# Seven block products for layer 0's attention output too, and one place for the attention weights, in a two-layer diffusion transformer kernel

## The chip, the cores and the metric

The kernel runs on one core of one Trainium2 chip. The metric is device microseconds for one execution. Before the change three runs took 2224.48, 2226.77 and 2225.25 us: the median is 2225.25 us. A core has five engines that run their own instruction queues side by side: TensorE (PE, with PEld for its weight loads), VectorE (DVE), ScalarE (ACT), GpSimd (POOL) and SyncE (SP), which issues all DMA transfers of this kernel. An instruction that waits for a semaphore holds up all that stands behind it on its engine.

## The reference

Two transformer layers over a batch of 16 items, each 256 rows of 256 numbers, all in fp32. Layer 0 (`D` = 256, 16 heads of 64) is self attention, cross attention over a context of 256 rows of 192, and a feed-forward net; each adds to `x`:

```python
attn_in = _adaln(x, cond, ln1_w, ln1_b, g1_w, g1_b, b1_w, b1_b)
x = _attn(attn_in, attn_in, sa_wq, sa_wkv, sa_wo, sa_bo) + x
cross_in = _adaln(x, cond, ln1_w, ln1_b, g1_w, g1_b, b1_w, b1_b)
ctx_n = _ln(context, ca_lnc_w, ca_lnc_b)
x = _attn(cross_in, ctx_n, ca_wq, ca_wkv, ca_wo, ca_bo) + x
ffn_in = _adaln(x, cond, ln2_w, ln2_b, g2_w, g2_b, b2_w, b2_b)
h = jax.nn.gelu(ffn_in @ ff_w1 + ff_b1, approximate=False)
x = h @ ff_w2 + ff_b2 + x
```

`_attn` projects to queries, keys and values of width 1024 (`MID`), turns queries and keys by a rotary embedding, takes softmax and sums over values, and ends with `o @ wo + bo`, where `o` is 256 x 1024 and `wo` 1024 x 256. That last product is what the change is about. Layer 1 does the same kinds of steps with heads of 16 and another modulation; there the attention output product is 256 x 256 by 256 x 256 and stays as it is.

## The kernel before

There are six phases: layer 0 self attention, cross attention and FFN, then the same three of layer 1. In each phase all 16 items are worked through, one after another; an item is a "job". An attention job has two steps (s = 0 and 1, eight heads each in layer 0), an FFN job four. The queues are in the order in which the kernel issues the instructions: no scheduler reorders them, and the program's tile framework adds the semaphores.

The loop over steps (from L861) writes the order by hand. In a layer 0 attention step it has, in this order: VectorE's partial sums of the exponentials (`stage_t`, tile `both`, L548; `stage_turn`, L554), TensorE's projections for the next step, called `rotary`, four pieces of which VectorE multiplies by the rotary table into the tiles `m` (L484) and POOL combines pairwise into `qk` (L492); then the sums over values (`layer0_sums`, L596), `stage_reduce` (L561), the rest of the previous job, the next job's values (`layer0_values`, L82 and L431) and at the end the next scores (`stage_s`, L527), whose exponentials ACT takes (L539). The tiles `m` have two buffers each, so VectorE's m for the second half of a step wait for POOL's qk of the first.

The previous job is called `late`. In step 0 its softmax sums are added up (`sum_up`), inverted, and sent through DRAM to be spread over partitions (tile `spread`); in step 1 POOL multiplies the job's four raw sums by them (`scale`, L585), and TensorE makes the output product (`finish`, L724, recorded at the helper's line L82): eight chunks by two row tiles into one PSUM bank, and one VectorE add into `x` (L738). PSUM has eight banks, addressed by number; rotary uses 0 to 3, the sums 4 and 5, values 6 and 7, scores 0 to 7, and `finish` bank 1. The next scores therefore begin, in bank 0, where rotary's products have been read.

The FFN's second product is 256 x 1024 by 1024 x 256 as well and is made by Strassen's scheme: `fold_weights` (L671) adds and subtracts blocks of the weight once a phase, `fold_hidden` (L684) makes five sums of blocks of the hidden activations on VectorE (L699), `finish_folded` (L701) does seven block products of 128 x 512 by 512 x 128 instead of eight, in two banks, and adds them into `x` with five VectorE instructions (L713 to L720). In each fp32 product a matrix instruction stands twice in the trace: 64 calls show as 128 records.

Weights lie in the pool `wpool`, two buffers for each of the tags `wq`, `wkv`, `wo`, `bo`. `load_phase` (L786) loads all weights of the next phase into the other buffers in step 1 of the first job of a phase (step 3 in an FFN).

Of the kernel before, what the change touches and what calls it, by code (L numbers as in the profile page):

```python
# [16 lines left out]
P = 128  # L17
# [26 lines left out]
def fast(ctx: ExitStack, tc: tile.TileContext, a: dict, out: bass.AP, flag):  # L44
# [166 lines left out]
    def wtile(shape, tag, name):  # L211
        return wpool.tile(shape, F32, tag=tag, name=name)

    def load_layer0_attention(kind, between=None):
        wq = wtile([P, KC, H * 64], "wq", f"wq_{kind}")
        wkv = wtile([P, 2, 2 * H * 64], "wkv", f"wkv_{kind}")
        wo = wtile([P, 8, D], "wo", f"wo_{kind}")
        halves = [slice(part * 512, (part + 1) * 512) for part in range(4)]

        def load_keys(cut):  # L220
            nc.sync.dma_start(out=wkv[:, :, cut], in_=chunked(a[f"{kind}_wkv"])[:, :, cut])

        def load_queries(cut):
            nc.sync.dma_start(out=wq[:, :, cut], in_=chunked(a[f"{kind}_wq"])[:, :, cut])

        load_keys(halves[0])
        load_queries(halves[0])
        if between is not None:
            between(0)
        load_keys(halves[2])  # L230
        load_keys(halves[3])
        if between is not None:
            between(1)
        load_queries(halves[1])
        load_keys(halves[1])
        bo = broadcast_row(a[f"L0_xcond_{kind}_bo"], "bo", f"bo_{kind}")
        nc.sync.dma_start(out=wo, in_=chunked(a[f"{kind}_wo"]))
        return {"wq": wq, "wk": wkv, "wv": wkv[:, :, H * 64 :], "wo": wo, "bo": bo}

    def load_layer1_self():  # L240
        w = wtile([P, KC, 3 * D], "wkv", "wqkv_b")
        nc.sync.dma_start(out=w, in_=chunked(a["L1_xcond_Wqkv"]))
        wo = wtile([P, KC, D], "wo", "wo_b1")
# [6 lines left out]
    def load_layer1_cross():  # L250
        w = wtile([P, 3, 2, D], "wkv", "wqkv_c")
# [3 lines left out]
        wo = wtile([P, KC, D], "wo", "wo_b2")  # L255
# [6 lines left out]
    def load_ffn(w1n, w2n, b1n, b2n, key):  # L262
        w1 = wtile([P, KC, 4 * D], "wq", f"w1_{key}")
        w2 = wtile([P, 8, D], "wo", f"w2_{key}")
        nc.sync.dma_start(out=w1, in_=chunked(a[w1n]))
        nc.sync.dma_start(out=w2, in_=chunked(a[w2n]))
        return {"w1": w1, "w2": w2, "b1": b1n, "bo": broadcast_row(a[b2n], "bo", f"bo_{key}")}
# [402 lines left out]

    def fold_weights(ph):  # L671
        w2 = ph["w"]["w2"]
        b = [[w2[:, 4 * k : 4 * k + 4, n * P : (n + 1) * P] for n in range(2)] for k in range(2)]
        folded = ph["folded"] = {2: b[0][0], 5: b[1][1]}
        for m, x, y, op in ((1, b[0][0], b[1][1], ALU.add), (3, b[0][1], b[1][1], ALU.subtract),
                            (4, b[1][0], b[0][0], ALU.subtract), (6, b[0][0], b[0][1], ALU.add),
                            (7, b[1][0], b[1][1], ALU.add)):
            folded[m] = (
                work.tile([P, 4, P], F32, tag="cT", name=f"folded_w_{m}") if m == 7 else
                work.tile([P, 4, P], F32, tag="qk", name=f"folded_w_{m}", bufs=4)  # L680
            )
            nc.vector.tensor_tensor(folded[m], x, y, op)

    def fold_hidden(job):  # L684
        a = [[job["halves"][k][:, :, t * P : (t + 1) * P] for k in range(2)] for t in range(2)]
        folded = job["folded"] = {3: a[0][0], 4: a[1][1]}
        sums = [
            (5, a[0][0], a[0][1], ALU.add), (2, a[1][0], a[1][1], ALU.add), (1, a[0][0], a[1][1], ALU.add),
            (7, a[0][1], a[1][1], ALU.subtract), (6, a[1][0], a[0][0], ALU.subtract),
        ]  # L690
        if job is jobs[-1]:
            sums = sums[4:] + sums[:4]
# [905 lines left out]
```

## Time and profile before

| What | Value |
|---|---|
| median of the runs | 2225.25 us (2224.48 to 2226.77) |
| profiled execution | 2226.61 us, of it span 2224.7 us |
| granted TensorE clock | 1.000 |
| one self attention job of layer 0 | 42.11 us (392.54 to 434.65) |
| one cross attention job of layer 0 | 39.37 us (884.84 to 924.21) |
| layer 0's two attention phases | about 31 to 1318 us of the span |
| POOL's scale, L585 | 128 instructions, 184.4 us, mean 1472 ns |
| VectorE's `both`, L548 | 256 instructions, 213.7 us; 624 / 684 / 1804 ns least, median, most |
| VectorE's FFN folds, L699 | 155 instructions, 674 / 683 / 879 ns |
| matrix product 128x32 by 128x256 | 379 ns in flight, four side by side |
| matrix product 128x32 by 128x128 | 273 ns in flight |

The page gives busy time for each engine, then the chain of waits that ended last, then groups of instructions by line. A group's mean can hide instructions that waited inside: `both` is one. The timeline lists an engine's instructions in order, equal neighbours merged ("x4"), with start and length in us; a remark in brackets tells how long the engine was idle before, and who released it. Matrix instructions overlap, so the time of a stretch of products is best taken from start to start.

### The profile page before, as it was taken

The numbers are of one execution on the slowest core, as the hardware profiler recorded it, in microseconds if no ns is written. First come the engines' busy times: TensorE is split into PE (matmuls) and PEld (weight loads), VectorE is DVE, ScalarE is ACT, GpSimd is POOL, SyncE is SP. The second block draws the span as 40 slices with busy tenths as digits, with TensorE's granted clock in tenths as the row PEclk, the third lists the DMA queues.
The fourth block names the chain that finished last, engine by engine and source line by source line (L and its number), as shares of the span: only waits on it lengthen the run. The fifth ranks groups of instructions, "written<-read, shape, count | busy, mean of one in ns | idle before, by whom it ended". The sixth has DMA issues, their size and how long they took to land.

```text
span 2224.7 us, 104669 instructions
## 1 busy us (share of the span) xinstructions
PE 2208.8 (99%) x47625; PEld 1401.1 (63%) x47625; DVE 1583.5 (71%) x2996; ACT 836.8 (38%) x1303; POOL 871.5 (39%) x873
## 2 busy tenths in 40 slices
PE   9999999999999999999999999999999999999998
PEld 5555555555555555555555567777665665657998
DVE  5777677677678787787878775564777777777654
ACT  2233233233233333333323332233666666663322
POOL 3445444445445546454554532121223322223220
PEclk9999999999999999999999999999999999999999
DMA  8110011111122221221212113211211232223221
GB/s 253 37 40 22 22 35 28 22 35 29 25 46 81 57 60 36 46 53 37 62 34 46 38 44 90 51 41 46 51 37 42 48 100 61 61 51 80 65 62 37
DMA packets 305678, 117.29 MB, mean 53 GB/s; under 512 B 242548, under 2 KB 288968, under 8 KB 305096
## 3 DMA queue, kind: packets, MB, share of 16 engines
q1 hardware_dynamic: 305224, 110.51, 20.5%
q8 instruction: 374, 6.13, 1.2%
q14 instruction: 80, 0.66, 0.1%
HBM read 77.14 MB, written 33.29 MB: 50 GB/s over the span
## 4 chain that ended last, share of the span: by engine, by line
PE 98%; POOL 1%; DVE 1%; issue 0%; ACT 0%; DMA 0%; SPq 0%; POOLq 0%; ACTq 0%; DVEq 0%
PE banks L82 64%; PE banks L527 16%; PE banks L596 10%; PE banks L612 5%; PE banks L463 2%; PE banks L431 1%; PE banks L171 0%; POOL raw L585 0%; DMA mod_a<-in_L_xcond_g_w 0%; POOL qk L492 0%; DVE m L484 0%; ACT pr L539 0%; DVE sums L638 0%; POOL oT L647 0%; ACT hT L356 0%
## 5 line engine op out<-in xcount | busy, mean ns | idle before, releaser
L539 ACT ACTIVATE pr<-banks 128x1024 f32<-128x1024 f32 x576 | 487.3, 938 | 220.8 <-PE banks L527 207.3
L492 POOL TENSOR_TENSOR qk<-m,m 128x512 f32<-128x512 f32 x256 | 347.0, 1376 | 370.5 <-DVE m L484 266.4
L484 DVE TENSOR_TENSOR m<-banks,rope 128x512 f32<-128x512 f32 x512 | 325.3, 681 | 89.0 <-POOL qk L492 74.2
L548 DVE TENSOR_TENSOR both<-pr 128x512 f32<-128x512 f32 x256 | 213.7, 844 | 75.0 <-ACT pr L539 73.7
L603 ACT COPY raw<-banks 128x512 f32<-128x512 f32 x128 | 75.0, 586 | 473.3 <-PE banks L596 400.7
L527 PE MATMUL banks<-qk 32*64 32x256 f32 x8192 | 238.7, 377 | 0.4 <-POOL qk L492 0.3
L527 PEld LDWEIGHTS banks<-qk 32*64 32x64 f32 x8192 | 184.4, 131 | 78.0 <-issue 44.0
L596 PE MATMUL banks<-pr,v 128*32 128x256 f32 x4096 | 233.4, 379 | 0.0
L662 ACT ACTIVATE g<-banks,cols 128x256 f32<-128x256 f32 x256 | 106.5, 470 | 278.3 <-PE banks L82 261.8
L436 ACT COPY v<-banks 128x512 f32<-128x512 f32 x128 | 71.8, 587 | 357.2 <-PE banks L431 178.8
L596 PEld LDWEIGHTS banks<-pr,v 128*32 128x32 f32 x4096 | 133.2, 110 | 88.5 <-ACT pr L539 0.7
L585 POOL TENSOR_TENSOR raw<-raw,spread 128x512 f32<-128x512 f32 x128 | 184.4, 1472 | 0.0
L554 DVE STREAM_TRANSPOSE squares<-both 128x1024 f32<-128x1024 f32 x128 | 159.1, 1243 | 3.4
L738 DVE TENSOR_TENSOR x<-banks,x 128x512 f32<-128x512 f32 x65 | 44.9, 691 | 158.9 <-PE banks L82 158.9
L561 DVE TENSOR_REDUCE rows<-squares 128x32 f32<-128x1024 f32 x128 | 155.4, 1214 | 2.2
L290 POOL TENSOR_TENSOR rstd<-ve,neg_half 128x2 f32<-128x2 f32 x95 | 67.0, 705 | 197.0 <-DVE ve L288 193.7
L82 PE MATMUL banks<-hT,wq_sa 128*32 128x256 f32 x2048 | 135.7, 381 | 2.3 <-issue 2.3
L82 PE MATMUL banks<-hT,wkv_sa 128*32 128x256 f32 x2048 | 136.2, 383 | 0.9 <-ACT hT L356 0.9
L612 PE MATMUL banks<-pr,wide_v 128*32 128x256 f32 x2048 | 134.4, 379 | 1.1 <-ACT pr L539 1.1
L82 PE MATMUL banks<-hT,wq_ca 128*32 128x256 f32 x2048 | 134.0, 379 | 0.0
L647 POOL TENSOR_TENSOR oT<-oT,spread 128x256 f32<-128x256 f32 x64 | 45.7, 735 | 209.9 <-DVE spread L646 209.9
L527 PE MATMUL banks<-q,k 32*64 32x256 f32 x4096 | 127.8, 381 | 0.0
(146 smaller groups left out, 3543.9 us busy)
## 6 DMA issues: line engine op xcount, KB each, us to landing
turned<-blocks SPq DMA_DIRECT2D x380, 64.0 KB
fetched<-turned SPq DMA_DIRECT2D x380, 64.0 KB
spread<-sums_seen SPq DMA_DIRECT2D x128, 128.0 KB
x<-in_x SPq DMA_DIRECT2D x16, 256.0 KB
fetched_c<-turned_c SPq DMA_DIRECT2D x64, 64.0 KB
cT<-in_ctx_turned SPq DMA_DIRECT2D x16, 256.0 KB
out<-x SPq DMA_DIRECT2D x16, 256.0 KB
ctx<-in_ctx SPq DMA_DIRECT2D x16, 192.0 KB
```

The source lines that it names most:

```text
L82: nc.tensor.matmul(out[cut], lhsT[:, cut], rhs, start=start, stop=stop)
L484: nc.vector.tensor_tensor(m, pq, rope[:, s : s + 1, :].to_broadcast([P, 2, N]), ALU.mult)
L492: nc.gpsimd.tensor_tensor(r, x, y, (ALU.subtract, ALU.add)[out])
L527: nc.tensor.matmul(banks[64 * g : 64 * g + 64, at + h, t * N : (t + 1) * N], lhs, rhs, start=(half == 0), stop=(half == 1 or job["layer"] ...
L539: nc.scalar.activation(pr[:, one], sc[:, one], AF.Exp, scale=0.125 if job["layer"] == 0 else 0.25)
L548: nc.vector.tensor_tensor(job["both"][:, 2 * p : 2 * p + 2, :], pr[:, :, 0, :], pr[:, :, 1, :], ALU.add)
L554: nc.vector.transpose(job["squares"].rearrange("p b k -> p (b k)"), job.pop("both").rearrange("p h n -> p (h n)"))
L561: nc.vector.tensor_reduce(job["rows"][:, u, :], job.pop("squares"), AX.X, ALU.add)
L585: nc.gpsimd.tensor_tensor(part, part, spread[:, u : u + 1, :].to_broadcast([P, 2, N]), ALU.mult)
L596: nc.tensor.matmul(o[32 * h : 32 * h + 32, half, :], v[:, t, col : col + 32], prs[h // 2][:, h % 2, t, :], start=(t == 0), stop=(t == NT - 1),
L612: nc.tensor.matmul(o[32 * h : 32 * h + 32], v[:, t, 4 * c + h, 32 * e : 32 * e + 32], prs[h // 2][:, h % 2, t, :], start=(t == 0), stop=(t ...
L662: nc.scalar.activation(g[:, c, :], ph[:, c, :], AF.Gelu, bias=column(w["b1"], 2 * u + c))
```

## The change

Layer 0's attention output product goes through `fold_weights` and `finish_folded` as well. The five folds of a job's sums are split: 5, 2 and 1 on POOL in step 0 of the next job, right after `scale`, which moves there from step 1; 7 and 6 on VectorE in step 1, between rotary's last two pieces. `finish_folded` uses banks 1 and 0 (7 and 6 in a phase's last job) and stands behind both of VectorE's reduces. An attention phase's weights are folded in step 0 of job 1, two on POOL and three on VectorE. The last cross attention job, which is finished inside the FFN, keeps `finish`.

The weights' tags become `wk`, `wq` and `wv` with one buffer each, shared by all phases; `wo` keeps two, and five folded weights get tiles of their own. Loads are in three parts: "early" (bias, output weights, modulation, all of layer 1's attention) in step 1 of job 1 (3 in an FFN), "values" at the start of step 0 of the phase's last job, "keys" (keys and queries, or the FFN's first weights) at the end of that step, ahead of the scores.

```diff
-    def load_layer0_attention(kind, between=None):
...
+    def load_layer0_attention(kind, part, between=None):
+        halves = [slice(i * 512, (i + 1) * 512) for i in range(4)]
+        wkv_src = chunked(a[f"{kind}_wkv"])
+        w = {}
+        if part == "keys":
+            w["wk"] = wtile([P, 2, H * 64], "wk", f"wk_{kind}")
+            w["wq"] = wtile([P, KC, H * 64], "wq", f"wq_{kind}")
+            for i, cut in enumerate(halves[:2]):
+                nc.sync.dma_start(out=w["wk"][:, :, cut], in_=wkv_src[:, :, cut])
+                nc.sync.dma_start(out=w["wq"][:, :, cut], in_=chunked(a[f"{kind}_wq"])[:, :, cut])
+                if between is not None and i == 0:
+                    between()
+        if part == "values":
+            w["wv"] = wtile([P, 2, H * 64], "wv", f"wv_{kind}")
+            for i in range(2):
+                nc.sync.dma_start(out=w["wv"][:, :, halves[i]], in_=wkv_src[:, :, halves[2 + i]])
+        if part == "early":
+            w["bo"] = broadcast_row(a[f"L0_xcond_{kind}_bo"], "bo", f"bo_{kind}")
+            w["wo"] = wtile([P, 8, D], "wo", f"wo_{kind}", 2)
+            nc.sync.dma_start(out=w["wo"], in_=chunked(a[f"{kind}_wo"]))
+        return w
...
     def fold_weights(ph):
-        w2 = ph["w"]["w2"]
...
-            nc.vector.tensor_tensor(folded[m], x, y, op)
+            if ph["kind"] == "attn":
+                folded[m] = wtile([P, 4, P], "folded", f"folded_w_{m}", 5)
...
+            (nc.gpsimd if ph["kind"] == "attn" and m < 4 else nc.vector).tensor_tensor(folded[m], x, y, op)
+
+    def fold_inner(job, eng, *which):
         a = [[job["halves"][k][:, :, t * P : (t + 1) * P] for k in range(2)] for t in range(2)]
...
+        folded = job.setdefault("folded", {3: a[0][0], 4: a[1][1]})
+        sums = {5: (a[0][0], a[0][1], ALU.add), 2: (a[1][0], a[1][1], ALU.add), 1: (a[0][0], a[1][1], ALU.add),
+                7: (a[0][1], a[1][1], ALU.subtract), 6: (a[1][0], a[0][0], ALU.subtract)}
+        for m in which:
+            folded[m] = work.tile([P, 4, P], F32, tag="folded", name=f"folded_{job['key']}_{m}", bufs=5)
+            eng.tensor_tensor(folded[m], *sums[m])
+
+    def finish_folded(job, at):
...
-        first, second = (bank(next_bank(), 4, P) for _ in range(2))
-        third = bank(next_bank(), 4, P) if final else second
+        first, second, third = (bank(i, 4, P) for i in (at if final else (*at, at[1])))
...
-        if s == (3 if ffn else 1) and job["b"] == 0 and job["p"] + 1 < len(phases):
-            load_phase(job["p"] + 1)
+        more = job["p"] + 1 < len(phases)
+        if s == 1 and job["b"] == (3 if ffn else 1) and more:
+            load_phase(job["p"] + 1, "early")
+        if s == 0 and job["b"] == NB - 1 and more:
+            load_phase(job["p"] + 1, "values")
...
-            if late is not None and s == 1:
-                scale(late)
...
             rotary(then, 1, 0)
+            if late is not None and s == 1:
+                fold_inner(late, nc.vector, 7, 6)
             rotary(then, 1, 1)
             for e in range(2):
                 layer0_sums(job, 2 * s + e, 4 + e if then else e)
             stage_reduce(job, 2 * s)
-            if late is not None and s == 1 and then:
-                finish(late, 1)
             stage_turn(job, 2 * s + 1)
             stage_reduce(job, 2 * s + 1)
-            if late is not None and s == 1 and not then:
-                finish(late, 7)
+            if late is not None and s == 1:
+                finish_folded(late, (1, 0) if then else (7, 6))
+            if late is not None and s == 0:
+                scale(late)
+                fold_inner(late, nc.gpsimd, 5, 2, 1)
+            if s == 0 and job["b"] == 1:
+                fold_weights(job["phase"])
...
+        if s == 0 and job["b"] == NB - 1 and more:
+            load_phase(job["p"] + 1, "keys")
         scores(i + 1)
```

The FFN's folds move to the new tiles too, in the order they had, and its first weights become the "keys" part of its phase.

## The prediction

> **What bounds the kernel now.** I read the page's busy shares and its chain of waits first, then the table by stretches for one item of each layer 0 attention phase, then the timeline of the steps that the change touches. Page:
>
> ```profile
> PE 2208.8 (99%) x47625; PEld 1401.1 (63%) x47625; DVE 1583.5 (71%) x2996; ACT 836.8 (38%) x1303; POOL 871.5 (39%) x873
> PE 98%; POOL 1%; DVE 1%; issue 0%; ACT 0%; DMA 0%; SPq 0%; POOLq 0%; ACTq 0%; DVEq 0%
> ```
>
> TensorE never waits in mid phase, so a shorter product shows in full unless another engine falls late. By stretches (one self attention item, one cross attention item; columns: length, then busy time of PE, PEld, DVE, ACT, POOL):
>
> ```profile
> 392.54:434.65 42.11, 42.11 (x844) 24.34 (x840) 29.41 (x44) 12.73 (x17) 19.51 (x16) 1.00 0.13 28
> 884.84:924.21 39.37, 39.37 (x796) 22.46 (x792) 31.13 (x53) 12.95 (x18) 20.98 (x18) 1.00 0.20 46
> ```
>
> VectorE is busy 70% of an item in self attention, 79% in cross attention: cross attention has less room. The timeline has the old product, the FFN's seven-product form of the same size, and the second step of a cross item:
>
> ```profile
> 1002.78 7.09 PE L82 MATMUL banks<-wo_ca,raw 128*32 128x256 f32 x128
> 1009.69 1.90 PE L82 MATMUL banks<-wkv_ca,cT 128*32 128x512 f32 x16
> ...
> 1350.58 1.93 PE L82 MATMUL banks<-w_a,folded 128*32 128x128 f32 x64
> 1352.33 1.93 PE L82 MATMUL banks<-folded_w,g 128*32 128x128 f32 x64
> 1354.08 2.80 PE L82 MATMUL banks<-folded_w,folded 128*32 128x128 f32 x96
> 1356.70 1.91 PE L82 MATMUL banks<-hT,w_a 128*32 128x256 f32 x32
> ...
> 987.26 2.52 POOL L492 TENSOR_TENSOR qk<-m,m 128x512 f32<-128x512 f32 x2 [1.49 <-DVE m L484]
> 993.89 5.65 POOL L585 TENSOR_TENSOR raw<-raw,spread 128x512 f32<-128x512 f32 x4
> 999.75 2.81 POOL L492 TENSOR_TENSOR qk<-m,m 128x512 f32<-128x512 f32 x2 [0.22 <-DVE m L484]
> ...
> 996.97 1.42 DVE L548 TENSOR_TENSOR both<-pr 128x512 f32<-128x512 f32 x1
> 999.51 0.67 DVE L548 TENSOR_TENSOR both<-pr 128x512 f32<-128x512 f32 x1
> 1001.36 2.53 DVE L484 TENSOR_TENSOR m<-banks,rope 128x512 f32<-128x512 f32 x4 [1.18 <-POOL qk L492]
> 1003.81 1.21 DVE L561 TENSOR_REDUCE rows<-squares 128x32 f32<-128x1024 f32 x1
> 1009.94 0.69 DVE L738 TENSOR_TENSOR x<-banks,x 128x512 f32<-128x512 f32 x1 [4.92 <-PE banks L82]
> ```
>
> Read three things. The old product takes 6.91 us (start to start). The FFN's seven products take 6.12 us. And POOL leaves the m buffers only when its qk pair runs, so VectorE's last four m wait for POOL; the `both` add takes 1.42 us instead of 0.67 us while POOL runs a two-input instruction.
>
> **The product.** 6.91 - 6.12 = 0.79 us for each of the 31 items that use the new form (self attention 0 to 15, cross attention 0 to 14; the last cross item keeps the old form). 31 x 0.79 = **24.5 us gained**.
>
> **The folds and the scaling, cross attention.** POOL's scale (4 instructions) moves from the second step to the first, ahead of it nothing but qk; behind it come three folds and the rstd pair, and only then the second step's qk. POOL's two-input 128x512 takes 1.26 us in qk, 1.47 us in raw beside VectorE, 1.24 us from start to start alone; the folds were never on POOL, so 1.24 to 1.47 us each, and I take 1.24 plus VectorE's turns. From 989.78 (end of qk): three scales to 993.55, `both` to 994.1, fourth scale to 995.25, `both` to 995.8, folds to 997.0, 998.2, 999.45, the third `both` to 1000.0. On VectorE: transpose to 997.05, m to 998.3, m after the third `both` to 1001.2. POOL's rstd pair ends 1001.3, so qk starts at 1001.4 (before: 999.75) and frees the first buffer at 1002.95. Then VectorE in its new order: two m 1.22, folds 7 and 6 (0.60 apart; 0.68 each in the FFN) 1.20, two m 1.2, reduce 1.24, transpose 1.28, reduce 1.14, that is 1010.3; then the five adds, which in the FFN take 2.35 us without waits: 1012.65. They read banks 1 and 0, and the next scores begin by writing bank 0. TensorE is ready at 1002.78 + 6.12 + 2.85 (values) = 1011.75, and must wait until 1012.7: **0.95 us per item**, which eats the 0.79. Queued behind the wait are the scores, ACT's exponentials and all of the next step, so it is paid in full: 13 steps (in cross items 0 and 3 to 14) x 0.95 = **12.4 us**. The one in item 2 has 1.9 us of modulation products as cover: 0.2. Bounds for one item: without contention 0; with folds at 1.47 us, 1.6.
>
> The row for that contention is `both` at 1.42 against 0.67 us: it waits 0.75 us. [...]
>
> **The same in self attention.** There POOL's qk ends 1.39 us before the scores instead of 0.36 us after them, values take 3.55, and the rstd is one. The same replay leaves qk's start at 388.6 (before 388.88), VectorE is done with its reduces at 397.6, before TensorE's product ends at 398.5; the last two adds end at 399.7 and the scores are ready to start at 402.0. 2.2 us of cover once VectorE's own chain is counted, so no cost; the cover is gone if POOL or VectorE comes more than that later.
>
> **The weights' folds** stand in the first step of item 1: two on POOL (2.5 us) and three on VectorE (0.6 to 1.23 us each: 1.8 to 3.7) behind the scale. They delay qk by 3.4 us (self) and 4.0 us (cross): 3.4 - 2.2 = 1.2 us, and 0.95 + 4.0 = 5.0. **6.2 us** (bounds 2 and 9: the instructions hidden as in the FFN, or each at its longest).
>
> **One place for the weights.** Loads now wait until the place is free. (a) Self to cross: the values' half goes out at about 664 in the last self item and lands some 5 us later, in time for 669.55. The keys' loads stand behind sums, spread and fetch on SP, which end at 673.8 before, and later by about 2.4 us since 1 MB is in front of them: first 512 KB issued at 676.2. Before, such a load landed 4.3 to 4.8 us after issue; the first use (cross keys, right after the scores) was at 676.04. Wait 680.5 - 676.04 = **4.5 us** (bounds 2.5 and 6). Queries come 1.3 us behind, as they are used. (b) Cross to FFN: 1 MB issued about 1304.5, needed at 1318: nothing. But POOL's folds there end after the scale that already held TensorE at 1314.16 (0.61 us): the last finish gains nothing, **1.0 us** with that. (c) Cross to FFN in layer 1: the load stands behind the four sums_seen issues, needed by the FFN's first product:
>
> ```profile
> 2001.94 2.49 SPq L642 DMA_DIRECT2D sums_seen<-sums  x4
> 2006.14 5.36 PE L82 MATMUL banks<-hT,w_b 128*32 128x256 f32 x96
> ```
>
> Issued at 2004.45. The FFN's 1 MB load of 715.64 moved its last bytes in the fifth microsecond and landed 5.2 us after issue: 2009.65, so **3.5 us** of idle TensorE (bounds 2.5 and 5). [...]
>
> SP's other moved loads (the output weights in item 1 of the phase before, 1 MB, no longer 4.5 MB in item 0) lie beside 40 us of work. The end of the kernel and the FFN's folds keep order and length; only their buffers change.
>
> **Sum.** -24.5 + 12.4 + 0.2 + 6.2 + 4.5 + 1.0 + 3.5 = +3.3 us. On the profiled execution, 2226.61 us (span 2224.7 and 1.9 around it), that is 2229.9; it lay 1.36 us over the median of the three runs, so **2228.5 us**.
>
> **Rivals.** (1) The cross attention chain is in time: if POOL's folds and `both` fall so that qk starts 1 us sooner, 12.4 us are saved: **2216**. For it: the chain misses by under 1 us in 22. Against: both POOL and VectorE reach 1001.3 on their own. (2) POOL's folds read strided halves and run slower, the trace has none like it: at 1.47 us (its mean raw) to 1.77 (its slowest qk) instead of 1.24 the chain is 0.6 to 1.6 us longer in cross attention, while self attention is still covered: 14 x 0.6 to 1.6 = 8 to 22 us more, **2237 to 2250**. It decides from folds of 1.34 us on. Against: qk and raw of equal size take 1.24 alone. (3) The loads are earlier than I think, SP not held up: 8 us fewer, **2221**. (4) The product does not shorten: against it, the FFN's identical 224 matrix products take 6.12 us; no chance of note.
>
> **How the numbers follow.** Forecast as reckoned 0.5, own range 2223 to 2235 (waits 0.6 to 1.3 us for 13 items, loads 5 to 11 us); rival 1 0.2; rival 2 0.2; rival 3 0.1. The range 2215 to 2239 holds the forecast, rivals 1 and 3 and the near part of 2. A measurement of this kernel tells about 0.2% (4.45 us) from no change: below 2220.8 is faster, above 2229.7 slower. Faster: 0.2 from rival 1 and 0.04 from 3. Same: 0.28 of the forecast, 0.06 of 3. Slower: 0.22 of the forecast and 0.2.
>
> **What the profile would show.** Right: groups of 128x128 products for wo at 6.12 us; a self attention item of 41.3 us; a cross item of 39.5 us with scores waiting on VectorE's last add; gaps of some 4 us ahead of the first cross keys and 3.5 us ahead of the second FFN. Wrong: cross items of 38.6 us (rival 1) or over 40 (rival 2), self items above 41.5, or no gap at the phase borders. Most likely to break it: POOL's time for a strided fold, and the landing of the first keys.

## The result, and the profile after

The changed kernel takes 2239.94 us (median of six runs, 2237.93 to 2242.78) against 2225.36 us before (six runs, 2223.26 to 2226.77): ratio 1.0067, 95% interval 1.0054 to 1.0080, **slower by 14.6 us**. The forecast was 2228.5 us, in a range from 2215 to 2239. The profiled execution took 2240.61 us, of it span 2238.8 us; before it was 2226.61 and 2224.7, so the two profiles differ by 14.1 us.

The page's busy shares and its chain, changed kernel:

```profile
PE 2192.0 (98%) x50601; PEld 1446.6 (65%) x50601; DVE 1721.4 (77%) x3188; ACT 837.6 (37%) x1303; POOL 998.4 (45%) x970
...
PE 79%; POOL 7%; DVE 7%; DMA 3%; issue 2%; SPq 1%; ACT 0%; POOLq 0%; DVEq 0%; ACTq 0%
```

TensorE works 16.8 us less than before and yet the span is 14.1 us longer: some 31 us of new idle time. The chain of the kernel before ran through TensorE for 98%, now for 79%; POOL, VectorE and transfers have taken the place. What TensorE waits for (columns: total us, times, longest; three short waits that both kernels have are left out):

```profile
PE banks L533 <- DVE x L721: 21.0, 15, 2.8
PE banks L469 <- DMA wk_ca<-in_ca_wkv: 4.7, 1, 4.7
PE banks L82 <- DMA w_b<-in_L_xcond_W: 3.2, 1, 3.2
PE banks L82 <- POOL rstd_c L296: 2.3, 1, 2.3
PE banks L82 <- POOL folded L700: 2.2, 2, 1.6
...
PE banks L602 <- DVE add_a L182: 1.0, 1, 1.0
```

None of these six waits was there before. The first is the handoff of banks 1 and 0 to the scores, which the prediction had at 12.4 us; the next two are the loads. The granted clock is the share of full speed at which TensorE was let run. Stretches of one item each, self attention item 9, then cross items 4, 6 and 12 (length, then busy us of PE, PEld, DVE, ACT, POOL, the granted clock, DMA share, GB/s):

```profile
395.66:436.98 41.32, 41.32 (x941) 26.29 (x937) 32.79 (x51) 12.73 (x17) 24.45 (x22) 1.00 0.12 29
854.22:893.94 39.72, 38.64 (x889) 24.79 (x889) 35.96 (x59) 13.03 (x20) 24.44 (x21) 1.00 0.21 46
934.00:974.40 40.40, 39.01 (x888) 24.76 (x875) 35.95 (x58) 12.99 (x19) 24.95 (x21) 1.00 0.21 46
1176.03:1219.16 43.13, 40.32 (x889) 26.26 (x889) 36.02 (x59) 13.12 (x18) 25.22 (x21) 0.96 0.19 43
```

Self attention is as predicted: 41.32 for 42.11 us, the whole 0.79. Cross attention took 39.37 us an item before, but for item 2, in which the modulation is made (41.40), and item 14 (39.65). Now the calm items take about 39.72 (items 13 and 14 39.6), and the others lie up to 3.9 us above that. VectorE is busy 36 us of such an item. (Items are counted from 0 in their phase; an item's time is taken from its first scores to the next item's. Item 6 begins 0.23 us ahead of the window shown and takes 40.63.)

The timeline of a calm item, cross item 4, second step:

```profile
870.78 4.99 POOL L591 TENSOR_TENSOR raw<-raw,spread 128x512 f32<-128x512 f32 x4
875.85 4.55 POOL L700 TENSOR_TENSOR folded<-raw,raw 128x512 f32<-128x512 f32 x3
880.36 0.69 POOL L296 TENSOR_TENSOR rstd<-ve,neg_half 128x2 f32<-128x2 f32 x1
...
882.44 2.85 POOL L498 TENSOR_TENSOR qk<-m,m 128x512 f32<-128x512 f32 x2 [0.72 <-PE banks L602]
...
881.02 1.28 DVE L490 TENSOR_TENSOR m<-banks,rope 128x512 f32<-128x512 f32 x2
...
893.37 0.42 DVE L721 TENSOR_TENSOR x<-banks,x 128x256 f32<-128x256 f32 x1
...
891.77 1.09 PE L437 MATMUL banks<-wv_ca,cT 64*64 64x512 f32 x8
893.94 3.71 PE L533 MATMUL banks<-qk 32*64 32x256 f32 x128 [1.08 <-DVE x L721]
```

In its ends this is the predicted chain, almost to the tenth. Counted from the end of the first step's qk (870.78; the prediction's 989.78) the prediction has qk at 882.4 and the last add's end at 893.65; the trace has 882.44 and 893.79. The scores wait 1.08 us. Inside, the pieces differ from the replay and make up for one another: the scale took 4.99 us and not 5.47, the three folds 4.55 and not 3.65, and VectorE's first two `both`, beside POOL, ended 1.2 us later than replayed. POOL was free at 881.72; qk started 0.14 us after VectorE's m, which it reads, had ended at 882.30, so the release that the remark puts down to TensorE was most likely VectorE's.

An item with a late transfer, cross item 12, same timeline:

```profile
1187.76 0.35 SPq L579 DMA_DIRECT2D sums_seen<-inv  x1
1191.14 1.74 SPq L582 DMA_DIRECT2D spread<-sums_seen  x4
...
1192.14 2.52 POOL L498 TENSOR_TENSOR qk<-m,m 128x512 f32<-128x512 f32 x2 [1.49 <-DVE m L490]
1195.97 5.97 POOL L591 TENSOR_TENSOR raw<-raw,spread 128x512 f32<-128x512 f32 x4 [1.31 <-DMA spread<-sums_seen]
...
1219.16 3.20 PE L533 MATMUL banks<-qk 32*64 32x256 f32 x105 [2.81 <-DVE x L721]
```

The spread loads were issued 3.4 us after the write of the sums, not 1.9 as in item 4; POOL could not start the scale for 1.31 us, and the next scores waited 2.81 us, 1.73 more than in item 4. In all POOL waited 13.3 us in 12 places for spread (none before), most of it in self attention, whose calm items still took 41.32. In cross items 9 to 12 it waited 0.25, 0.53, 1.00 and 1.31 us, and the scores that followed waited 1.30, 1.56, 2.13 and 2.81. The trace of before had the same jitter, where it cost nothing because the scale came a step later:

```profile
1061.61 0.35 SPq L573 DMA_DIRECT2D sums_seen<-inv  x1
1064.84 1.74 SPq L576 DMA_DIRECT2D spread<-sums_seen  x4
...
1140.37 0.35 SPq L573 DMA_DIRECT2D sums_seen<-inv  x1
1141.86 1.74 SPq L576 DMA_DIRECT2D spread<-sums_seen  x4
```

3.2 us from issue to issue in one item, 1.5 in another. The border from self to cross attention, changed kernel:

```profile
664.40 0.40 SPq L224 DMA_DIRECT2D wk_ca<-in_ca_wkv  x1
...
660.50 3.71 PE L533 MATMUL banks<-qk 32*64 32x256 f32 x128
668.90 1.99 PE L469 MATMUL banks<-cT,wk_ca 64*64 64x256 f32 x16 [4.70 <-DMA wk_ca<-in_ca_wkv]
670.82 1.08 PE L82 MATMUL banks<-cT,wk_ca 128*32 128x256 f32 x8
```

The wait is as predicted. What was not: the products behind it run at half speed (1.99 us, where the same 16 take 1.09 inside the phase). The granted clock has a window of 0.5 from 668.5 to 671.9 us, and two more at 1177.1 and 1323.9, each 3.413 us long. The kernel before had none until its end, where both kernels have one.

### The profile page after: what moved, and what is told of

It reads as the page before. It is cut to its first block, busy times and chain, and to the rows that moved or that the text cites. A ratio compares the mean times of both kernels' runs of the same rounds, so it can differ in the third digit from the quotient of the medians.

```text
span 2238.8 us, 110884 instructions
## 1 busy us (share of the span) xinstructions
PE 2192.0 (98%) x50601; PEld 1446.6 (65%) x50601; DVE 1721.4 (77%) x3188; ACT 837.6 (37%) x1303; POOL 998.4 (45%) x970
## 4 chain that ended last, share of the span: by engine, by line
PE 79%; POOL 7%; DVE 7%; DMA 3%; issue 2%; SPq 1%; ACT 0%; POOLq 0%; DVEq 0%; ACTq 0%
PE banks L82 53%; PE banks L533 14%; PE banks L602 6%; PE banks L618 5%; POOL raw L591 3%; DVE m L490 2%; POOL folded L700 2%; POOL qk L498 1%; DMA spread<-sums_seen 1%; DVE rows L567 1%; PE banks L469 1%; DMA sums_seen<-inv 1%; SPq L582 1%; DVE squares L560 1%; DVE folded L700 1%
## 5 line engine op out<-in xcount | busy, mean ns | idle before, releaser
L554 DVE TENSOR_TENSOR both<-pr 128x512 f32<-128x512 f32 x256 | 236.7, 932 | 93.0 <-ACT pr L545 92.8
L533 PEld LDWEIGHTS banks<-qk 32*64 32x64 f32 x8192 | 192.1, 132 | 96.8 <-issue 51.5
L591 POOL TENSOR_TENSOR raw<-raw,spread 128x512 f32<-128x512 f32 x128 | 172.4, 1381 | 14.0 <-DMA spread<-sums_seen 13.3
L82 PE MATMUL banks<-folded_w,folded 128*32 128x128 f32 x5952 | 174.2, 273 | 0.0
L82 PEld LDWEIGHTS banks<-folded_w,folded 128*32 128x32 f32 x5952 | 163.9, 110 | 0.0
L296 POOL TENSOR_TENSOR rstd<-ve,neg_half 128x2 f32<-128x2 f32 x95 | 74.2, 781 | 142.1 <-DVE ve L294 138.8
L82 PE MATMUL banks<-hT,wk_sa 128*32 128x256 f32 x2048 | 136.4, 384 | 0.9 <-ACT hT L362 0.9
L700 POOL TENSOR_TENSOR folded<-raw,raw 128x512 f32<-128x512 f32 x93 | 134.0, 1467 | 2.4
```

The lines of the kernel that those rows point to most:

```text
L82: nc.tensor.matmul(out[cut], lhsT[:, cut], rhs, start=start, stop=stop)
L533: nc.tensor.matmul(banks[64 * g : 64 * g + 64, at + h, t * N : (t + 1) * N], lhs, rhs, start=(half == 0), stop=(half == 1 or job["layer"] ...
L554: nc.vector.tensor_tensor(job["both"][:, 2 * p : 2 * p + 2, :], pr[:, :, 0, :], pr[:, :, 1, :], ALU.add)
L591: nc.gpsimd.tensor_tensor(part, part, spread[:, u : u + 1, :].to_broadcast([P, 2, N]), ALU.mult)
L700: eng.tensor_tensor(folded[m], *sums[m])
```

## The experiments

Differences of time are between medians; ratios are to the kernel before, which ran beside each group of kernels at 2224.9 to 2225.9 us. Diffs are against the changed kernel unless said otherwise.

### 1. Which part loses it

**Other banks for the product.**

```diff
-                finish_folded(late, (1, 0) if then else (7, 6))
+                finish_folded(late, (4, 5) if then else (7, 6))
```

> The changed kernel with one edit: the seven products of a late job go to banks 4 and 5 instead of 1 and 0, so that the next scores reach the two banks in their second half, some 1.7 us after their start, and not with their first instruction. Nothing else moves: POOL's scale and folds, VectorE's chain and its five adds stay as late as they are. Theory A (the loss in cross attention is the handoff of the two banks: TensorE waited 21.0 us in 15 waits of its scores for VectorE's last add, and another 2 to 4 us of slow scores followed those waits): waits up to 1.7 us vanish, the three longer ones leave 2.3 us in all, cross items settle at 38.6 us instead of 39.7 to 43.1, the kernel takes about 2219 us (2215 to 2223). Theory B (VectorE and POOL cannot keep up in cross attention, so a wait removed in one place comes back at the next): cross items stay at 39.3 us or more, the wait turns up at another line, the kernel takes 2233 us or more. Theory C (the product itself with its 224 instead of 128 calls is what costs, whatever bank it uses): no change, 2240.

Measured 2223.86 us, ratio 0.999 (0.9981 to 1.0000): 16 us less than the changed kernel, 0.9 above the span of theory A.

```profile
PE banks L533 <- DVE x L721: 1.8, 6, 0.3
```

The waits for the last add shrink from 21.0 to 1.8 us, and cross items 3 to 5 take the full 38.6 us. So the handoff is where the loss shows. From item 6 on, items lie between 38.8 and 40.1 us, because VectorE's adds still hold banks 4 and 5 in the middle of the scores. That is no steady lag: it follows POOL's wait for spread in the item before. After waits of 0.22, 0.83, 1.10, 1.16 and 1.24 us the scores took 0.35, 1.05, 1.33, 1.48 and 1.51 us longer (one wait of 1.25 gave only 0.91). Theory A for most of it; C is out. On the mean items 3 to 14 take 39.21 us, 0.16 less than with the old product.

**Earlier loads.**

```diff
             rotary(then, 1, 1)
+            if s == 0 and job["b"] == NB - 1 and more:
+                load_phase(job["p"] + 1, "keys")
...
-        if s == 0 and job["b"] == NB - 1 and more:
+        if not layer0 and not ffn and s == 0 and job["b"] == 3 and job["cross"]:
             load_phase(job["p"] + 1, "keys")
```

> The changed kernel with its keys loads moved and nothing else: in layer 0 they are issued right behind the last rotary product that reads the old weights, ahead of the fetches, instead of at the end of that step; the last FFN's first weights are issued in step 0 of item 3 of layer 1's cross attention, since their place has been free from the first FFN on. Theory A (TensorE's 4.7 us wait for the cross keys and its 3.2 us wait for the last FFN's weights are queue positions on SP, and the half clock of 3.4 us behind the first gap costs another 1.5 us): both waits gone, the half clock at the first border gone, some 1.6 us of the second wait had been made up later anyhow, so 7 to 8 us less: 2232 us (2230 to 2235). Theory B (the loads would land no earlier, since the fetches and the transfers share the engines, or the fetches behind them now come late): 2237 or more, with a wait of the next input for its fetch.

Measured 2237.24 us (1.0051, 1.0034 to 1.0068): 2.7 us less, not 8. The last FFN's wait is gone, the one for the cross keys is down to 2.0 us, still with a window of half clock behind it. But cross items 9 and 10 came out 1.2 and 2.5 us longer than in the changed kernel's trace, items 0 to 14 together 4.4 us, and further windows of half clock stood at 759, 1093 and 1179 us. While cross attention is that uneven, it hides what a change elsewhere is worth; the loads are priced again below.

**Seven products in self attention alone, and none at all** (the second has `()` in place of `(0,)`; POOL's and VectorE's folds carry the same condition):

```diff
+            whole = late is not None and late["p"] not in (0,)
+            if whole and s == 1:
+                scale(late)
...
             stage_reduce(job, 2 * s)
+            if whole and s == 1 and then:
+                finish(late, 1)
...
-            if late is not None and s == 1:
+            if late is not None and s == 1 and not whole:
                 finish_folded(late, (1, 0) if then else (7, 6))
```

> The changed kernel with the seven products in self attention alone; cross attention items get the old product in bank 1 and POOL's scale in the second step as before. Loads and weight places stay as changed. Theory A (self attention gains its 0.79 us per item, cross attention is where it is lost): self items 41.32 us, cross items 39.37 us but for the first, whose late job is still folded; 11.9 us gained in self attention, 6.1 lost on loads and the half clock at the border to cross attention, 0.7 in the first cross item, 1 to 2.5 at the border to the FFN, 1.6 in layer 1's FFN: about 2222 us (2219 to 2225). Theory B (the loss comes from the one place of the weights and the lower clock, and the cross items' share is small): 2232 or more.

> The one place for the weights alone: no job of either attention phase is folded, both keep the old product and the old scale; the new tags and load times stay. Theory A (the loads cost two waits and a half clock, and the shorter start gives back 1.8 us): 4.7 + 1.5 at the border to cross attention, about 1 at the border to the FFN, 3.2 less 1.6 in layer 1, less 1.8 at the start: 2232 us (2229 to 2235). Theory B (the loads alone cost nothing, because without the folds everything around them is earlier): 2225 us, no wait of TensorE for a weight in the trace.

Self attention alone: 2225.64 us (1.0003, 0.9993 to 1.0013), 0.6 above the span of theory A. Self items 41.32, cross items from 3 on 39.37, as theory A has it; but the border cost 8.2 us (a wait of 5.6 and 6.8 us of half clock) where I had 6.1, and another window of half clock stood at the last FFN. The place alone: 2236.95 us (1.0048, 1.0032 to 1.0065), **11.2 us lost with no seven products anywhere**. Its waits:

```profile
PE banks L469 <- DMA wk_ca<-in_ca_wkv: 6.8, 1, 6.8
PE banks L82 <- DMA w_b<-in_L_xcond_W: 4.3, 1, 4.3
```

Behind each come 6.8 us of half clock. Its first border costs 9.4 us and its last FFN 5.9, the start gains 2.5. That is 2 us over the span expected. So the loads cost more than the prediction had for them, and part of it comes through the clock.

### 2. Can the order mend it

**POOL's folds behind the second step's first qk pair.**

```diff
             rotary(then, 0, 1)
+            if late is not None and s == 1:
+                fold_inner(late, nc.gpsimd, 5, 2, 1)
...
                 scale(late)
-                fold_inner(late, nc.gpsimd, 5, 2, 1)
...
-        places = {5: first[:, 0], 2: first[:, 1], 4: first[:, 2], 3: first[:, 3],
+        places = {4: first[:, 2], 3: first[:, 3], 5: first[:, 0], 2: first[:, 1],
```

> The changed kernel with POOL's three folds moved from the first step, behind the scale, to the second step, behind the first pair of qk; the seven products are issued in the order 4, 3, 5, 2, 1, 7, 6, so that those of unfolded sums come first. Banks 1 and 0, the loads and the weights' folds stay. Theory A (the folds on POOL ahead of the second step's qk make VectorE's chain late, and with it the handoff, the slow scores behind it and the lower clock): the scores' waits for VectorE's last add vanish but for item 1, cross items 38.6 us from item 3 on, item 1 about 40, the kernel 2214 us (2210 to 2219). Theory B (the late landing of spread, 13.3 us of waits on POOL, is what makes the chain late; the folds only come on top): cross items stay uneven, on the mean above 39.0 us, waits of the scores of 5 us or more remain, the kernel 2222 us or more.

Measured 2251.75 us (1.0119, 1.0102 to 1.0136): a clear miss, 12 us slower. The folds now come too late for the product itself:

```profile
PE banks L82 <- POOL folded L700: 19.1, 32, 2.1
PE banks L533 <- DVE x L721: 9.0, 15, 1.5
```

The first qk pair waits for VectorE's m, so the folds start only when TensorE begins the products, and three of them take longer than the products of unfolded sums last. One wait was traded for another, and the handoff came back behind it.

**All cures, and two of them undone.** Of this kernel's edits the folds' order and the banks are shown above; further:

```diff
             if s == 1 and job["b"] == 0:
+                fold_weights(job["phase"])
...
                 layer0_values(nxt, s)
+            if s == 1 and job["b"] == NB - 2:
+                load_phase(job["p"] + 1, "values")
```

> All cures together: POOL's folds behind the second step's first qk pair and the products in the order 4, 3, 5, 2, 1, 7, 6; products in banks 4 and 5; the weights' folds at the end of item 0; the values' load right behind the last values product that reads the old ones, the keys' and queries' load right behind the last rotary product, the last FFN's first weights during layer 1's cross attention; in the last item of cross attention the old product, with the scale staying in the first step. Theory A (the seven products gain 0.79 us an item wherever nothing else is late): 30 items by 0.79 = 23.7 us and 2 us of shorter start, less up to 3 us of loads that are still short: 2202 us (2198 to 2208). Theory B (part of the loss is owed to the larger number of matrix instructions, 224 for 128 a product, and no order of the other engines removes it): cross items above 38.8 us without any wait of TensorE for another engine, 2210 us or more.

> The kernel with all cures, but the loads back where the change has them. It prices the one place for the weights on its own. Theory A (two waits of 4.7 and 3.2 us, and windows of half clock of 1.5 us each behind them, as in the run of the place alone, where both together cost 14 us at the two borders): 9 to 14 us more than with all cures, about 2213 us (2210 to 2217). Theory B (a later chain hid part of it, or the start's gain depends on it): less than 6 us more.

> The kernel with all cures, but the weights' folds back in the first step of item 1. It prices them: 0.74 us in self attention as measured in the changed kernel (0.05 gained instead of 0.79), and in cross attention the 4.0 us by which they delay POOL and VectorE, less about 1.5 to 3 us that the later folds and the other banks leave as room. Theory A: item 1 of cross attention 39.6 to 41 us, in all 2 to 4 us more than with all cures. Theory B (with the folds behind qk they are covered): same within 0.5 us.

All cures: 2222.14 us (0.9988, 0.9978 to 0.9997), far from the 2202 expected.

```profile
PE banks L82 <- POOL folded L700: 16.2, 30, 1.2
```

No load is waited for and the clock is full until the kernel's end, but TensorE waits for POOL's folds, about 1 us in a cross item: the miss of the run before again, whose result these expectations did not have. Old loads: 2235.41, **13.3 us more**, within the 9 to 14 of theory A. This is the price of where the change issues its loads; the one place for the weights is in the kernel with all cures too, and there no load is waited for. Old weights' folds: 2225.37, 3.2 us more, within the 2 to 4 expected; cross item 1 pays 3.0 of it. At 44.58 us that item lies well above the 39.6 to 41 expected; a window of half clock falls into it.

**POOL's folds split,** against the kernel with all cures:

```diff
             stage_turn(job, 2 * s)
+            if late is not None and s == 1 and not whole:
+                fold_inner(late, nc.gpsimd, 5)
             rotary(then, 0, 0)
...
-                fold_inner(late, nc.gpsimd, 5, 2, 1)
+                fold_inner(late, nc.gpsimd, 2, 1)
```

> The kernel with all cures, with POOL's three folds split: fold 5 at the start of the second step, in the 3.2 us in which POOL waits there for VectorE's m, folds 2 and 1 behind the first qk pair as before. Nothing else moves. Theory A (the 16.2 us that TensorE still waits in 30 places for POOL's folds, 1.2 us in each cross item, are there only because all three stand behind qk): the waits go, cross items 38.6 us, 2222 less 13 times 1.2: 2206 us (2202 to 2211). Theory B (fold 5 ahead of qk makes qk and VectorE's chain late again): the scores wait for VectorE's last add or its adds hold banks 4 and 5, cross items 39 us or more, 2214 us or more.

Measured 2216.12 us (0.9957, 0.9944 to 0.9971): 6.0 us better, 10 short of the forecast.

```profile
PE banks L82 <- POOL folded L700: 5.3, 11, 0.6
```

The waits for folds fall from 16.2 to 5.3 us, but in nearly every cross item the first scores now take 0.59 us longer, held in their middle, where banks 4 and 5 begin. Cross items 3 to 13 lie between 38.95 and 40.02 us, 39.64 on the mean. No complete kernel here brings all of cross attention to 38.6. The old product's 39.37 was beaten only by the order of the first experiment (folds in the first step, banks 4 and 5), and there by 0.16 us an item. That order together with the early loads and the weights' folds at the end of item 0 was not run.

### 3. Folds or landings

> The changed kernel without POOL's folds 5, 2 and 1 in cross attention: the products 5, 2 and 1 take unfolded sums in their place, so this leaves part of the computation out; self attention is whole. TensorE, VectorE and all loads do the same work in the same order. Theory A (the folds' 3.7 to 4.5 us on POOL ahead of the second step's qk are the cause of the loss in cross attention): waits of the scores for VectorE's last add vanish but for the first item, whose late job is a folded one, and item 1; the others 38.6 us; 2215 us (2212 to 2219). Theory B (the late landing of spread makes the chain late by itself): cross items on the mean above 39.0, 2222 us or more.

```diff
+                    late["folded"].update({5: late["folded"][3], 2: late["folded"][4], 1: late["folded"][3]})
```

> The changed kernel with the scale multiplying by a constant table in place of spread: the transfers are still made, but POOL waits for none of them. This leaves the division by the sums out. Theory A (the folds are the main cause, the landings account for what is uneven): no wait of POOL for a transfer, all cross items from item 3 on at the 39.72 us of the even ones, 6 to 8 us less than the changed kernel: 2233 us (2230 to 2235). Theory B (the landings are the main cause): cross items 38.6 to 39.0, 2222 us or less.

```diff
-            nc.gpsimd.tensor_tensor(part, part, spread[:, u : u + 1, :].to_broadcast([P, 2, N]), ALU.mult)
+            nc.gpsimd.tensor_tensor(part, part, rope[:, 0:1, :].to_broadcast([P, 2, N]), ALU.mult)
```

Without POOL's folds: 2219.57 us (0.9972, 0.9961 to 0.9983), 20 us less than the changed kernel and just past the end of the span expected. Cross items 3, 4 and 10 to 14 take 38.6 us; of the waits for the last add four are left: one in self attention, two at the ends of cross items 0 and 1, and one of 0.2 us. Without the landings: 2236.59 us (1.0053, 1.0038 to 1.0069), by the medians 3.4 us less than the changed kernel, with intervals that overlap; its profiled execution is 6.4 us shorter than the changed kernel's. The waits for the last add without the folds, then without the landings:

```profile
PE banks L533 <- DVE x L721: 5.3, 4, 2.5
...
PE banks L533 <- DVE x L721: 16.1, 15, 1.4
```

Without the landings there are still 15 waits, but none over 1.4 us; of cross items 4 to 13 seven lie between 39.70 and 39.90 us, two at 40.1, one at 39.6. So the folds' share of POOL's time makes every item late by 1.1 us, and the landings make it uneven: with them gone, the first and items 3 to 14 lose 15.4 us where the changed kernel loses 22.1. Of these 6.7 us, 3.0 are longer waits at the ends of items 10 to 12, 1.7 half clock behind one of them, and 1.6 lie in items 6 and 7, 1.4 of it in pauses of TensorE, which come next. That the folds are the cause is shown; how much the landings add rests on one profile of each kernel.

### 4. Holes in the scores, and the version that wins

In the changed kernel the scores of cross items 6, 7 and 8 last 0.4 to 0.7 us longer than the usual 3.71 without a wait for an engine in them. Item 7's first scores, then its second step's, by the timeline:

```profile
974.40 4.39 PE L533 MATMUL banks<-qk 32*64 32x256 f32 x128 [1.28 <-DVE x L721]
991.32 3.71 PE L533 MATMUL banks<-qk 32*64 32x256 f32 x128
```

TensorE's records simply stop for up to 0.5 us (a "hole"), at record 229, 241 and 253 of the 256 (loads and matrix instructions) of these scores. From one hole to the next are 1792 records, seven times 256. The run without POOL's folds has such holes where the scores had not waited for more than 0.2 us, at records 217, 229, 241 and 253.

```diff
     idle_products(1)
+    for _ in range(15):
+        nc.tensor.matmul(bank(0, 32), ident, ident[:, 0:32], start=True, stop=True)
```

> The changed kernel with 15 idle matrix calls of 32 columns at its start, which write a bank that nothing reads; they shift all later records of TensorE by 60 and change nothing else. In the changed kernel the scores of cross items 6, 7 and 8 have a hole of 0.2 to 0.5 us at record 229, 241 and 253 of their 256, where multiples of 256 records of TensorE's stream fall, counted from one hole to the next. Theory A (a block of 16 KB of TensorE's instructions is not there in time, when a block ends late in the scores behind the seven products): the holes leave items 6 to 8 and come at records 217 to 253 of the scores of items 10 to 13. Theory B (they are an after effect of the wait for the banks, or of the clock, in these items): they stay in items 6 to 8. Time 2240 us, up to 4 us more for the idle calls.

2241.69 us (two runs). The holes left items 6 to 8 and came at record 229 of item 11 and 253 of item 13 (217 in item 10 and 241 in item 12 had none). First scores of items 7, 11 and 13:

```profile
978.20 3.71 PE L535 MATMUL banks<-qk 32*64 32x256 f32 x128 [1.36 <-DVE x L723]
...
1137.86 4.08 PE L535 MATMUL banks<-qk 32*64 32x256 f32 x128 [1.58 <-DVE x L723]
...
1218.03 4.12 PE L535 MATMUL banks<-qk 32*64 32x256 f32 x128 [1.44 <-DVE x L723]
```

The changed kernel's item 10, 0.28 us longer at its last records, has its like in item 15 here. So these pauses follow the position in the instruction stream and not the item: theory B is out. That a block of instructions comes late, the reason in theory A, is not shown by it. Position alone does not make a hole either: the run without the landings has the same stream and none in items 6 and 7.

**Self attention alone, cured,** against the kernel with split folds: `whole` holds for all of cross attention, whose scale and product return to their old places.

```diff
-            whole = late is not None and late["p"] == 1 and late["b"] == NB - 2
+            whole = late is not None and late["p"] == 1
+            if whole and s == 1:
+                scale(late)
...
+            if whole and s == 1 and then:
+                finish(late, 1)
```

> Seven products in self attention alone, with the cures of the loads and of the weights' folds, POOL's folds split and banks 4 and 5; cross attention items have the old product and the old place of the scale. Theory A (cross attention has no room for the folds, so what it does with seven products is a loss even in the best order measured, 0.3 us an item against the old form; without them and with loads in time the 0.79 us of self attention stay whole): 14.1 us gained up to the border to cross attention as in the kernel with split folds, 0.2 lost in the first cross item, cross items 39.37 us, 1 us gained behind: 2210 us (2207 to 2214). Theory B (the last FFN or the border costs as much as in the run with self attention alone): 2217 us or more.

Measured **2210.80 us** (2209.91 to 2212.06), ratio 0.9937 (0.9923 to 0.9951): as expected, and better than both kernels. The page, then the stretches of a self and a cross item:

```profile
PE 2195.8 (99%) x49161; PEld 1402.3 (64%) x49161; DVE 1660.3 (75%) x3095; ACT 836.2 (38%) x1303; POOL 938.3 (42%) x923
...
PE 97%; DVE 1%; POOL 1%; issue 0%; DMA 0%; ACT 0%; SPq 0%; POOLq 0%; DVEq 0%; ACTq 0%
```

```profile
395.00:436.32 41.32, 41.32 (x952) 26.29 (x942) 33.48 (x49) 12.73 (x17) 23.68 (x20) 1.00 0.13 30
840.59:879.97 39.38, 39.38 (x797) 22.46 (x793) 31.13 (x53) 12.96 (x18) 20.98 (x18) 1.00 0.21 46
```

TensorE is the chain again, with no load waited for. The expectation's ground, that seven products are a loss in cross attention "even in the best order measured", holds for the split folds but not for the run with other banks, whose calm items gained; whether cross attention can pay stays open.

## Why the prediction was wrong, step by step

It was wrong by 11.4 us, just past the upper end of its range. The forecast's terms against the two profiles (item by item, between first scores; the product's 0.79 us is taken for every item, and what an item lacks of it stands in the rows below):

| Step of the prediction | predicted us | measured us |
|---|---|---|
| product, 31 x 0.79 | -24.5 | -24.5 |
| handoff in cross attention, 13 items | +12.4 | +22.1 |
| item 2 of cross attention | +0.2 | +1.2 |
| weights' folds, item 1 of both phases | +6.2 | +6.0 |
| border self to cross | +4.5 | +6.1 |
| last cross items and border to the FFN | +1.0 | +3.3 |
| last FFN's load | +3.5 | +1.9 |
| start, and the rest | 0 | -2.1 |
| sum | +3.3 | +14.0 |

- **The product: right.** 0.79 us in each of self attention's undisturbed items, and in cross attention wherever nothing waits (38.58 us for 39.37, with other banks or without the folds).
- **Self attention has cover: right.** 41.32 us against 41.3 predicted.
- **The handoff: the mechanism right, the term mis-sized.** This is the step that failed. "13 steps x 0.95" measured 22.1 us. A calm item such as item 4 loses 1.14, not 0.95; its last add ends 0.14 us later than in the replay, which is close partly by luck, since the pieces inside were off by up to 1.2 us and made up for one another. That would have made 14.8. The other 7.3 us are unevenness, which the step left out by replaying one item, in which POOL could start its scale at the end of qk, and multiplying by 13. The runs show the landings of spread for most of it (these items are 6.7 us shorter in the profile without them, half clock included) and the holes (1.8 us in items 6 to 8); the two overlap, as the holes of items 6 and 7 are gone without the landings. The lines of before shown above held the warning: the transfer that the scale needs was issued up to 1.7 us later in some items than in others, and the change took away the step of time that hid it.
- **Item 2: another wait.** The cover by the modulation's products held: the scores at the item's end wait for nothing. But TensorE waits 1.0 us in the item's middle for `add_a`, VectorE's sums for that modulation. They stand behind `both` adds that take 2.37 us (two) and 1.78 us beside POOL, and nobody waited for them before.
- **The weights' folds: right in size**, 1.0 in self attention and 5.0 in cross. The cross item pays in two places: 2.5 us at the scores, where it was predicted, and 2.3 us at the product itself. The wait list names `rstd_c` for the latter, which that product does not read; VectorE's m, which empties bank 1, ended 0.1 us ahead of it, and with banks 4 and 5 this wait is gone (there 1.8 us for VectorE's folds stand in its place).
- **The loads: waits right (4.7 for 4.5, 3.2 for 3.5), the price of a wait wrong.** No term stood for the clock behind it, some 1.5 us each at the two borders of layer 0. The 3.2 us at the last FFN were partly made up by the end, 1.3 us; where stays open.
- **The last cross items: mis-sized.** POOL's folds hold the last folded product by 2.2 us in two waits, and a window of half clock follows at 1323.9 us.
- **The start: 1.8 us gained, not in the sum.** The change loads in another order there; what of it gains was not tested.
- **The rivals.** Rival 2 named the right time (2237 to 2250) for a reason that was not there: POOL's strided folds take 1264 ns at least and 1287 in the middle, like qk of the same size (1265 and 1287); only the mean, 1467 (up to 1800), is over its limit of 1.34 us, so some folds are slower and most are not, which a strided view does not explain. Rival 1 (the chain in time) came true only where the folds were left out. Rival 3 (loads cheaper) went the other way.

## What to carry to other kernels

When an instruction moves a step earlier, look up the spread of its inputs' arrival over all items, not the arrival in one: slack that nobody used hides jitter, and the change spends it. Here 4.55 us of folds on POOL ahead of the second step's qk made the next scores of a calm cross item wait 1.08 us. Moving that work behind traded one wait for another here, while banks that are needed later took away most of the loss; ask first how much room the stage has (self attention hid the same folds; before the change its qk ended 1.39 us ahead of the scores, and in cross attention 0.36 us behind their start). A wait of TensorE cost more than its length here where half clock followed it: one late load at the border to cross attention, a wait of 4.7 to 6.8 us, cost 6.1 to 9.4 us, as much as eight to twelve items gain.

## What the runs showed of the hardware

- **Half clock after short waits.** Ahead of a kernel's end, windows of 0.5 clock lasted 3.413 us or twice that; the place alone paid 9.4 us at its border for a wait of 6.8. The changed kernel's three windows and the one at its end start 149, 43 and 267 times 3.4133 us apart. The length of a wait alone did not decide: the window at 1177.1 us followed a wait of 2.13 us, while waits of 2.48 us that ended at 772.7, of 2.81 us at 1219 and of 3.21 us at 2021.7 had none behind them. Cut by a grid of 3.4133 us through the starts of the windows, the wait of 2.13 us lies in one piece; the others fall into 0.74 and 1.74, 1.72 and 1.09, and 1.71 and 1.50 us. In this trace half clock followed the three pieces of the grid in which TensorE had idled 3.41, 2.22 and 2.13 us, and none of the other pieces up to the kernel's end, in which it had idled 1.82 us or less. So whether a wait of 2.1 to 3.2 us cost half clock on top hung here on where it fell on that grid.
- **TensorE can pause without a wait.** The holes of items 6 to 8 lie 1792 records apart, seven times 256, and the changed kernel's page counts 397 packets and 6.50 MB in the instruction queue, 16 KB each. In the kernel before, all scores of cross attention but the last took 3.71 us. With 224 instead of 128 matrix instructions ahead of them some took longer, by up to 1.1 us in the run without POOL's folds; most did not, and with all cures none in items 0 to 14. That a late transfer of such a packet makes the holes was not shown, only that they move with the stream.
- **The time from a small write to the reads behind it varied.** From the issue of the sums' write, 16 KB, to that of spread's reads 1.5 to 3.4 us passed within one phase of the kernel before.
